# Two graph layers on one core: decoding edge counts in pairs, with the weights stored by parity of the node

## The chip, the core and the metric

The kernel runs on one core of one Trainium2 chip. A core has TensorE (matmuls into PSUM), VectorE, ScalarE, GpSimd, SyncE (which issues most of the DMAs) and 16 DMA engines. The metric is the device time of one execution in microseconds, from the first to the last work on the chip; the smaller, the better. The time before is the median of three runs.

## The reference

There are N = 3327 nodes with D = 64 features, and a symmetric 0/1 matrix `adj` with about 16 edges in a row. Two layers follow each other, each with a layer norm and a relu in front and a residual sum behind it.

```python
h = relu(layernorm(x))
# layer 0: hyperbolic attention over the edges
att = sigmoid(left[:, None] + right[None, :] + b) * adj
support[i] = sum_j att[i, j] * logmap(h[i], h[j])
x = x + proj(expmap(h, support))
# layer 1: each row's edges are weighted by how many edges stand behind them in the row
h = relu(layernorm(x)); support = h @ weight
rank = cumsum(adj != 0, axis=1); deg = rank[:, -1:]; k = min(deg, 100)
w = mask * where(rank - (deg - k) > 0, 0.5 ** (deg - rank), 0)
x = x + w @ support + bias
```

So an edge's weight in layer 1 is a power of two whose exponent is a count: the number of edges behind it in its row. The last edge of a row has weight 1, the one before it 1/2, and so on.

## The kernel before

**Tiles.** The nodes are padded to 3328, that is 26 blocks of 128. A node j (the source of an edge) lies on a partition, 128 nodes of block j at a time; the nodes i (the rows of the result) lie along the free dimension. Layer 0 walks over four strips of i, with 8, 8, 6 and 4 blocks (1024, 1024, 768 and 512 columns), and inside a strip over the 26 blocks j from the last to the first. A round works on 1024 elements per partition at most: one block j in the first three strips, two in the fourth.

**A round of layer 0.** SyncE loads the part of the adjacency (`ad`). TensorE forms the pair products in PSUM (`products`, L670 and L671), ScalarE puts them through two gelus (`gelus`, L857 and L858) and makes the attention by a tanh (`sigmoids`, L653), and VectorE joins them (`pair_one`, L658, and `pair_two`, L663). TensorE sums the result over j (`total`, L680).

**The counts.** Beside that, in the same rounds, VectorE makes a 0/1 mask of the edges (`edges`, L620), and TensorE counts the edges behind each place in one PSUM tile that goes on from block to block (`count`, L631 and L632). `read` then takes the count out of PSUM, clips it at zero and keeps it. A count is one byte, in `behind_lo` (blocks 0 to 11) and `behind_hi` (blocks 16 to 25). The four blocks of `JD` (12 to 15) are different: their counts are multiplied by 128 at once and kept as 16 bit words in `weight_of`. A word of 128 * count, read as a bfloat16, has the count as its exponent, so it is the weight itself, up to a fixed power of two. `ON_ACT` says which reads ScalarE takes (L642); VectorE takes the others (L644 for the blocks of `JD`, L646 otherwise).

**Behind the strips.** After each strip a chain of small steps (`post`, in `per_node`) closes layer 0 for its nodes: sums, roots by GpSimd's power operation, the tanh, the new `x_sb`, the layer norm, and at its end the features `s2` (L1147, L1149) that layer 1 multiplies with. For the first three strips GpSimd does the small steps while the next strip runs; for the last strip VectorE does them (all recorded at L1044), during layer 1. The chain is a generator that yields after each step with a cost; `advance(LAST)` lets it go on by 8 units for each block of layer 1.

**Layer 1.** `weights` takes the blocks j in the order 12 to 15, 0 to 11, 16 to 21, and last the four blocks 22 to 25 that belong to the last strip. `decode` turns a block's 128 x 3328 bytes into words: ScalarE by a copy with a factor of 128 (L1285), VectorE by a product with 128 (L1287), in turn. It runs four blocks ahead of the matmuls (`LEAD`), into seven buffers `wt`. For each block `add` (L1299) makes seven matmuls, one for each chunk of 512 columns (the last has 256), with `s2` as the weights of the array, into seven PSUM tiles `pw`. For the last four blocks the order turns: chunk by chunk, all four blocks. Behind each chunk, ScalarE or VectorE copies `pw` to `ow` (L1340, L1342), and two chunks later `close` multiplies it by the layer's weight matrix (`w2s`, L1328), adds `x_sb` (which holds the bias already, L1304) and sends 512 rows out by a DMA.

**Order.** The order of work on TensorE, VectorE and ScalarE is the order in which the program issues it (`manual_schedule(engines=IN_ORDER)`): an instruction that waits holds up all that stands behind it on its engine. GpSimd and the DMAs on SyncE's queue follow their own orders. A branch to a general version of the kernel (not taken here) stands at the end.

Of the kernel before, what the change touches and what calls it, by code (L numbers as in the profile page):

```python
# [11 lines left out]
F32 = mybir.dt.float32  # L12
F16 = mybir.dt.float16
BF16 = mybir.dt.bfloat16
I32 = mybir.dt.int32
U16 = mybir.dt.uint16
U8 = mybir.dt.uint8
AF = mybir.ActivationFunctionType
ALU = mybir.AluOpType
# [3 lines left out]
P = 128  # L23
N = 3327
NB = 26
NP = NB * P
D = 64
# [3 lines left out]
JD = range(12, 16)  # L31
# [9 lines left out]
ROUND = (3.5, 3.5, 2.8, 1.9)  # L41

LEAD = 4

GSTRIPS = [(0, 7), (7, 7), (14, 6), (20, 6)]
GFMAX = 7 * P
# [35 lines left out]
def halves(n):  # L82
    return [(a, min(a + 512, n)) for a in range(0, n, 512)]
# [363 lines left out]
def fast(ctx, tc, x, adj_t, r, w_att, b_att, weight, bias, out, flag):  # L447

    nc = tc.nc
    V, A, G, T = nc.vector, nc.scalar, nc.gpsimd, nc.tensor  # L450
    const = ctx.enter_context(tc.tile_pool(name="f_const", bufs=1))

    x_sb = const.tile([P, NB, D], F32, name="x_sb")
# [14 lines left out]
    w2s = const.tile([P, D], F32, name="w2s")  # L468
# [67 lines left out]
    weight_of = const.tile([P, len(JD), NP], U16, name="weight_of")  # L536
    s2 = const.tile([P, NB, 2, D], F16, name="s2")
# [7 lines left out]
    def behind(j):  # L545
        if j in JD:
            return weight_of[:, j - JD.start]
        return behind_of["lo"][:, j] if j < JD.start else behind_hi[:, j - JD.stop]
# [53 lines left out]
    def span(n):  # L602
        k, lo, hi = rounds[n]
        return (hi - lo) * strips[k].F
# [17 lines left out]
    def count(n, j):  # L622
# [9 lines left out]
            T.matmul(S.pc[:, f0:f1], cb, now[:, f0:f1], start=S.first, stop=True, skip_group_check=True)  # L632
        S.before, S.first = now, False

    def read(n, j, on_act=None):
        k, lo, hi = rounds[n]
        S = strips[k]
        kept = behind(j)[:, S.i0 : S.i0 + S.F]
        num, den = ON_ACT[k]
        i = NB - 1 - j  # L640
        if on_act or (on_act is None and i * num // den != (i + 1) * num // den):
            A.activation(kept, S.pc[:, : S.F], AF.Relu, scale=128.0 if j in JD else 1.0)  # L642
        elif j in JD:
            V.tensor_scalar(kept, S.pc[:, : S.F], 0.0, 128.0, op0=ALU.max, op1=ALU.mult)  # L644
        else:
            V.tensor_scalar(kept, S.pc[:, : S.F], 0.0, None, op0=ALU.max)  # L646

# [58 lines left out]
    d, rl, sq, sr = (pre.tile([P, NB, D], F32, name=n) for n in ("d", "rl", "sq", "sr"))  # L706
# [3 lines left out]
    for hs in node_halves:  # L710
        n = hs.stop - hs.start
# [166 lines left out]
    for j in js(0):  # L878
        read(0, j, True)
# [10 lines left out]
    for b in (24, 20, 16, 12, 8, 4, 0):  # L890
        n = min(4, NB - b)
# [23 lines left out]
    for j in js(1):  # L915
        read(1, j, True)
# [251 lines left out]
    def per_node(k, pa):  # L1168
        nb = STRIPS[k][1]
        agg = post_pool.tile([P, nb, D + 1], F32, name="agg_last" if k + 1 == len(STRIPS) else "agg")  # L1170
        for c in range(0, nb, 4):
            m = min(4, nb - c)
            to, of = agg[:, c : c + m], pa[:, c * P : c * P + m * (D + 1)].rearrange("p (b d) -> p b d", b=m)
            if c == 0:
                V.tensor_copy(to, of)
            else:
                A.copy(to, of)
        return post(agg, k)
# [5 lines left out]
    def advance(portions):  # L1184
        for stage in stages:
            while portions > 0 and not stage.asked:
                portion = next(stage.portions, LATER)
                stage.asked = portion == ACT
                if portion >= LATER:
                    break  # L1190
                portions -= portion

    def asked_of_act():
        for stage in stages:
            if stage.asked:
                next(stage.portions)
                stage.asked = False

    def finish():
        for stage in stages:  # L1200
            for _ in stage.portions:
                pass
        stages.clear()
# [5 lines left out]
    for n in range(2, R):  # L1209
        k, lo, hi = rounds[n]  # L1210
        m, w = n + AHEAD, span(n)
# [22 lines left out]
        if n == 2:  # L1234
            for j in js(2):
                read(2, j, True)
# [33 lines left out]

    late = STRIPS[-1][0]
    order = [*JD, *range(JD.start), *range(JD.stop, late)]
    chunks = halves(NP)
    with tc.tile_pool(name="l1", bufs=2, reuse_waits="tile") as l1, tc.manual_schedule(engines=IN_ORDER):
        decoded = 0

        def decode(j):

            nonlocal decoded
            if j in JD:  # L1280
                return behind(j)
            wt = l1.tile([P, NP], U16, name="wt", bufs=7)
            decoded += 1
            if decoded % 2:
                A.activation(wt, behind(j), AF.Copy, scale=128.0)  # L1285
            else:
                V.tensor_scalar(wt, behind(j), 128.0, None, op0=ALU.mult)  # L1287
            return wt

        every = [*order, *range(late, NB)]  # L1290
        weights = {j: decode(j) for j in every[: len(JD) + 1]}
        stages.append(Stage(per_node(len(STRIPS) - 1, pa)))
        sums.close()
        l1_ps = ctx.enter_context(tc.tile_pool(name="l1_ps", bufs=1, space=PSUM, reuse_waits="tile"))
        pw = [l1_ps.tile([P, f1 - f0], F32, name=f"pw{n}") for n, (f0, f1) in enumerate(chunks)]

        def add(j, wt, n):
            f0, f1 = chunks[n]
            T.matmul(pw[n], s2[:, j].rearrange("p c d -> p (c d)"), wt[:, f0:f1].bitcast(BF16),  # L1299
                     start=j == order[0], stop=j == NB - 1)  # L1300

        def bias(b0, nb):
            xb = x_sb[:, b0 : b0 + nb]
            G.tensor_add(xb, xb, bias_b[:, None, :].to_broadcast([P, nb, D]))  # L1304

        for i, j in enumerate(order):
            for jn in every[: i + 1 + LEAD]:
                if jn not in weights:
                    weights[jn] = decode(jn)
            asked_of_act()  # L1310
            advance(LAST)
            for n in range(len(chunks)):
                add(j, weights[j], n)
            if i % 4 == 3 and i < STRIPS[-2][0]:
                bias(i - 3, 4)
        finish()
        bias(STRIPS[-2][0], late - STRIPS[-2][0])
        bias(late, NB - late)
        for j in range(late, NB):
            if j not in weights:  # L1320
                weights[j] = decode(j)
        ow = [l1.tile([P, 512], F32, name="ow", bufs=4)[:, : f1 - f0] for f0, f1 in chunks]

        def close(n):
            f0, f1 = chunks[n]
            b0, nb = f0 // P, (f1 - f0) // P
            for b in range(nb):
                T.matmul(pw[n][:, b * D : (b + 1) * D], ow[n][:, b * P : (b + 1) * P], w2s, start=True, stop=True)  # L1328
            o = l1.tile([P, 4, D], F32, name="o", bufs=4)
            V.tensor_add(o[:, :nb], pw[n][:, : nb * D].rearrange("p (b d) -> p b d", d=D), x_sb[:, b0 : b0 + nb])  # L1330
            full = nb if b0 + nb < NB else nb - 1
            nc.sync.dma_start(out[f0 : f0 + full * P, :].rearrange("(b p) d -> p b d", p=P), o[:, :full])
            if full < nb:
                nc.scalar.dma_start(out[f0 + full * P : N, :], o[: N - f0 - full * P, full])

        for n in range(len(chunks)):
            for j in range(late, NB):
                add(j, weights[j], n)
            if n % 2:
                A.copy(ow[n], pw[n])  # L1340
            else:
                V.tensor_copy(ow[n], pw[n])  # L1342
            if n > 1:
                close(n - 2)
        close(len(chunks) - 2)
        close(len(chunks) - 1)


@with_exitstack
def gnn_kernel(  # L1350
    ctx: ExitStack,
    tc: tile.TileContext,
    x: bass.AP,
    adj_t: bass.AP,
    r: bass.AP,
    w_att: bass.AP,
    b_att: bass.AP,
    weight: bass.AP,
    bias: bass.AP,
    out: bass.AP,  # L1360
):
    keep = ctx.enter_context(tc.tile_pool(name="keep", bufs=1))
    flag = keep.tile([1, 1], I32, name="flag")
    args = (x, adj_t, r, w_att, b_att, weight, bias, out)
    with ExitStack() as inner:
        fast(inner, tc, *args, flag)
    cond = tc.nc.values_load(flag)
    with tc.If(cond > 0):
        with ExitStack() as inner:
            general(inner, tc, *args)  # L1370
# [28 lines left out]
```

## Time and profile before

| | before |
|---|---|
| median of 3 runs (lowest, highest) | 416.37 us (414.42, 418.77) |
| the profiled execution: its time / its span | 418.25 us / 416.4 us |
| mean granted TensorE clock | 0.969 |
| busy: TensorE / VectorE / ScalarE / GpSimd | 361.1 / 373.1 / 364.8 / 124.0 us |
| first matmul of layer 1 | at 360.26 us |
| decodings: ScalarE / VectorE | 11 of 2.96 us / 11 of 1.89 us |
| reads of a `JD` block with 1024 columns: ScalarE / VectorE | 1.01 / 1.21 us |
| end of the last matmul / last output DMA issued | about 409.2 / 409.8 us |

The span runs from the first to the last instruction of the profiled execution. Times in the profile are microseconds unless marked ns. "PE" is TensorE's matmuls, "PEld" its loads of array weights, "DVE" VectorE, "ACT" ScalarE, "POOL" GpSimd, "SP" SyncE. A row gives the line in the kernel, the operation, what is written and what is read, and a shape. An idle time is given with the work that ended it. The chain of work that ended last is followed back from the last instruction. The granted clock is the share of full speed that TensorE had. Ends of matmuls are modelled.

### The profile page before, as it was taken

What the parts mean: (1) busy time and instruction counts of PE and PEld (TensorE: products, weight loads), DVE (VectorE), ACT (ScalarE), POOL (GpSimd) and SP (SyncE); (2) the same over time, 40 slices, a digit from 0 to 9 for tenths busy, and PEclk for the clock granted to TensorE, in tenths of its full rate; (3) what the DMA queues carried; (4) which work ended last, traced back from release to release, by engine and by line L of the source; (5) the groups of instructions that cost most, each with busy time, mean ns of one, the idle gap of its engine ahead of it and who ended that gap; (6) DMA issues with size and microseconds to landing.
All of it is one profiled execution on the core that took longest, in us unless ns stands there. A gap on an engine that the chain in (4) does not pass through costs nothing.

```text
span 416.4 us, 4699 instructions
## 1 busy us (share of the span) xinstructions
PE 361.1 (87%) x1436; PEld 154.4 (37%) x1460; DVE 373.1 (90%) x546; ACT 364.8 (88%) x411; POOL 124.0 (30%) x240
## 2 busy tenths in 40 slices
PE   0088999999997999999997999999777999899793
PEld 0063333333333333333333444444332333344352
DVE  4999799999999899999999798899989899898841
ACT  3589999999998899999999899999996999788810
POOL 8154200000000263930250163801405183452400
PEclk9998999999999899999999899999898999999987
DMA  7315544545466534554437255454643420000012
GB/s 218 123 40 143 161 148 147 158 145 161 146 186 181 152 107 148 153 151 109 145 113 178 94 153 151 119 146 128 186 117 104 114 87 0 2 0 0 2 25 65
DMA packets 23298, 48.99 MB, mean 118 GB/s; under 512 B 8789, under 2 KB 9245, under 8 KB 23265
## 3 DMA queue, kind: packets, MB, share of 16 engines
q1 hardware_dynamic: 20993, 47.66, 39.2%
q10 hardware_dynamic: 1808, 0.46, 0.6%
q0 software_dynamic: 464, 0.49, 0.5%
q8 instruction: 13, 0.21, 0.2%
q14 instruction: 20, 0.16, 0.1%
HBM read 46.40 MB, written 0.87 MB: 114 GB/s over the span
## 4 chain that ended last, share of the span: by engine, by line
DVE 33%; ACT 27%; PE 24%; issue 10%; POOL 3%; DMA 1%; DVEq 0%; POOLq 0%; ACTq 0%
DVE sg L663 9%; PE po L680 9%; ACT sg L653 8%; DVE sg L658 8%; ACT pq L857 8%; ACT pq L858 3%; DVE wt L1287 3%; PE pq L670 3%; PE pq L671 3%; DVE behind_lo L646 3%; PE pc L632 2%; PE pc L631 2%; ACT behind_lo L642 2%; ACT behind_hi L642 2%; PE pw L1299 2%
## 5 line engine op out<-in xcount | busy, mean ns | idle before, releaser
L680 PE MATMUL po<-sg,hw 128*65 128x512 f32 (+1 forms) x364 | 164.5, 576 | 0.5 <-DVE st L972 0.4
L663 DVE SCALAR_TENSOR_TENSOR sg<-pq,sg 128x1024 f32<-128x1024 f32 (+1 forms) x91 | 103.4, 1137 | 6.7 <-ACT pq L858 5.9
L658 DVE SCALAR_TENSOR_TENSOR sg<-sg,ad 128x1024 f32<-128x1024 f32 (+1 forms) x91 | 103.8, 1141 | 0.3
L653 ACT ACTIVATE sg<-left_b,right 128x1024 f32<-128x1024 f32 (+2 forms) x103 | 99.5, 979 | 0.0
L857 ACT ACTIVATE pq<-pq 128x1024 f32<-128x1024 f32 (+1 forms) x91 | 87.1, 957 | 3.5 <-PE pq L671 3.2
L858 ACT ACTIVATE pq<-pq 128x1024 f32<-128x1024 f32 (+1 forms) x91 | 86.2, 947 | 2.9
L680 PEld LDWEIGHTS po<-sg,hw 128*65 128x65 f32 x364 | 50.4, 141 | 71.3 <-issue 57.5
L631 PE MATMUL pc<-mask,ca 128*128 128x512 bf16 (+1 forms) x170 | 62.1, 365 | 11.1 <-DVE behind_hi L646 3.9
L670 PE MATMUL pq<-iu,ju 71*128 71x512 f16 (+1 forms) x182 | 68.2, 375 | 2.4 <-ACT jz L794 1.0
L671 PE MATMUL pq<-iz,jz 128*128 128x512 f16 (+1 forms) x182 | 67.2, 376 | 0.0
L632 PE MATMUL pc<-mask,cb 128*128 128x512 bf16 (+1 forms) x168 | 60.1, 368 | 2.2 <-ACT behind_lo L642 1.7
L620 DVE TENSOR_SCALAR mask<-ad 128x1024 bf16<-128x1024 f32 (+1 forms) x91 | 58.6, 645 | 0.0
L1044 POOL TENSOR_TENSOR dots<-dots,ih 128x8 f32<-128x8 f32 (+1 forms) x3 | 2.2, 720 | 134.3 <-DVE dots L1064 134.3
L1299 PE MATMUL pw<-wt,s 128*128 128x512 bf16 (+1 forms) x150 | 33.6, 374 | 4.3 <-DVE s L1149 2.2
L632 PEld LDWEIGHTS <-cb 128*128 128x128 bf16 x182 | 17.9, 98 | 51.7 <-issue 39.8
L631 PEld LDWEIGHTS <-ca 128*128 128x128 bf16 x175 | 17.3, 99 | 29.9 <-issue 17.8
L670 PEld LDWEIGHTS <-ju 71*128 71x128 f16 x182 | 18.1, 99 | 24.2 <-DVE sg L663 5.8
L1299 PEld LDWEIGHTS <-s 128*128 128x128 f16 x182 | 18.0, 100 | 23.6 <-issue 4.2
L642 ACT ACTIVATE behind_hi<-pc 128x1024 uint8<-128x1024 f32 (+2 forms) x25 | 21.8, 872 | 5.3 <-remote 3.3
L671 PEld LDWEIGHTS <-jz 128*128 128x128 f16 x182 | 18.2, 100 | 19.7 <-issue 3.3
L1304 POOL TENSOR_TENSOR x_sb<-x_sb,bias_b 128x256 f32<-128x256 f32 (+1 forms) x6 | 9.9, 1657 | 51.6 <-DVE w L1133 46.0
L642 ACT ACTIVATE behind_lo<-pc 128x1024 uint8<-128x1024 f32 (+2 forms) x29 | 24.9, 859 | 0.0
(313 smaller groups left out, 369.0 us busy)
## 6 DMA issues: line engine op xcount, KB each, us to landing
ad<-in_adj_t SPq DMA_DIRECT2D x65, 512.0 KB, 3.7
ad<-in_adj_t SPq DMA_DIRECT2D x26, 384.0 KB, 3.2
out<-o SPq DMA_DIRECT2D x6, 128.0 KB, 1.9
left_b<-left_d SPq DMA_DIRECT2D x1, 512.0 KB, 4.6
x_sb<-in_x ACTq DMA_DIRECT2D x1, 416.0 KB, 5.6
x_sb<-in_x SPq DMA_DIRECT2D x1, 416.0 KB
left_b<-left_d SPq DMA_DIRECT2D x1, 384.0 KB
jz<-iz POOLq DMA_DIRECT2D x2, 128.0 KB, 2.6
```

The source lines that it names most:

```text
L631: T.matmul(S.pc[:, f0:f1], ca, S.before[:, f0:f1], start=False, stop=True, skip_group_check=True)
L632: T.matmul(S.pc[:, f0:f1], cb, now[:, f0:f1], start=S.first, stop=True, skip_group_check=True)
L642: A.activation(kept, S.pc[:, : S.F], AF.Relu, scale=128.0 if j in JD else 1.0)
L653: A.activation(part(n, sg, j), S.left[:, : S.F], AF.Tanh, bias=right[:, j : j + 1], scale=0.5)
L658: V.scalar_tensor_tensor(sg, sg, 1.0, ad_of.pop(n)[:, :w], op0=ALU.add, op1=ALU.mult)
L663: V.scalar_tensor_tensor(sg, pq_of.pop(n)[:, :w], WD, sg, op0=ALU.add, op1=ALU.mult)
L670: T.matmul(part(n, pq, j, f0, f1), ju[:KB, j, :], S.iu[:, f0:f1], start=True, stop=False)
L671: T.matmul(part(n, pq, j, f0, f1), jz[:, j, :], S.iz[:, f0:f1], start=False, stop=True)
L680: T.matmul(S.po[: D + 1, f0:f1], hw[:, j, :], part(n, sg_of[n], j, f0, f1), start=j == NB - 1, stop=j == 0)
L857: A.activation(pq, pq, AF.Gelu, scale=-WG / QS)
L858: A.activation(pq, pq, AF.Gelu, scale=WH)
L1299: T.matmul(pw[n], s2[:, j].rearrange("p c d -> p (c d)"), wt[:, f0:f1].bitcast(BF16), start=j == order[0], stop=j == NB - 1)
```

## The change

**Layout by parity.** A row of 3328 weights is now stored as two halves of 1664: first the even nodes i, then the odd ones (`by_parity`). This holds for `weight_of`, which `read` writes in layer 0 from the same counts in PSUM, and for the buffers `wt`.

**Decoding.** VectorE takes two neighbouring bytes as one 16 bit word. One instruction keeps the low byte and shifts it left by 7, which gives the words of the even nodes; a second one keeps the high byte and shifts it right by 1, which gives those of the odd nodes. ScalarE still makes all 3328 words in one instruction, with a source that steps by two bytes. ScalarE now takes one decoding in three (`ACT_DECODES`), so 8 of the 22, and VectorE takes 14.

**Chunks.** The seven chunks of layer 1 keep their sizes, but the first six are now (q, r): the nodes of parity r among the 1024 nodes of group q. The seventh holds both parities of the last 256 nodes. After the sums, `copied` puts the results back in the order of the nodes: the even ones by VectorE, the odd ones by ScalarE, each with a step of two in its destination `kept_of`. `close` then works on a group of 1024 nodes and so waits for both of its chunks.

```diff
@@ -41,6 +41,7 @@
 ROUND = (3.5, 3.5, 2.8, 1.9)
 
 LEAD = 4
+ACT_DECODES = 3
 
 GSTRIPS = [(0, 7), (7, 7), (14, 6), (20, 6)]
 GFMAX = 7 * P
@@ -632,16 +633,23 @@
             T.matmul(S.pc[:, f0:f1], cb, now[:, f0:f1], start=S.first, stop=True, skip_group_check=True)
         S.before, S.first = now, False
 
+    def by_parity(t):
+        return t.rearrange("p (r k) -> p r k", r=2)
+
     def read(n, j, on_act=None):
         k, lo, hi = rounds[n]
         S = strips[k]
         kept = behind(j)[:, S.i0 : S.i0 + S.F]
         num, den = ON_ACT[k]
         i = NB - 1 - j
+        of = S.pc[:, : S.F]
+        if j in JD:
+            kept = by_parity(weight_of[:, j - JD.start])[:, :, S.i0 // 2 : (S.i0 + S.F) // 2].rearrange("p r k -> p k r")
+            of = of.rearrange("p (k r) -> p k r", r=2)
         if on_act or (on_act is None and i * num // den != (i + 1) * num // den):
-            A.activation(kept, S.pc[:, : S.F], AF.Relu, scale=128.0 if j in JD else 1.0)
+            A.activation(kept, of, AF.Relu, scale=128.0 if j in JD else 1.0)
         elif j in JD:
-            V.tensor_scalar(kept, S.pc[:, : S.F], 0.0, 128.0, op0=ALU.max, op1=ALU.mult)
+            V.tensor_scalar(kept, of, 0.0, 128.0, op0=ALU.max, op1=ALU.mult)
         else:
             V.tensor_scalar(kept, S.pc[:, : S.F], 0.0, None, op0=ALU.max)
 
@@ -1270,7 +1278,8 @@
 
     late = STRIPS[-1][0]
     order = [*JD, *range(JD.start), *range(JD.stop, late)]
-    chunks = halves(NP)
+    chunks = [(q, r) for q in range(3) for r in range(2)] + [(3, None)]
+    widths = [512] * 6 + [256]
     with tc.tile_pool(name="l1", bufs=2, reuse_waits="tile") as l1, tc.manual_schedule(engines=IN_ORDER):
         decoded = 0
 
@@ -1281,10 +1290,13 @@
                 return behind(j)
             wt = l1.tile([P, NP], U16, name="wt", bufs=7)
             decoded += 1
-            if decoded % 2:
-                A.activation(wt, behind(j), AF.Copy, scale=128.0)
+            to = by_parity(wt)
+            if decoded % ACT_DECODES == 1:
+                A.activation(to, behind(j).rearrange("p (k r) -> p r k", r=2), AF.Copy, scale=128.0)
             else:
-                V.tensor_scalar(wt, behind(j), 128.0, None, op0=ALU.mult)
+                pairs_of = behind(j).bitcast(U16)
+                V.tensor_scalar(to[:, 0], pairs_of, 0xFF, 7, op0=ALU.bitwise_and, op1=ALU.logical_shift_left)
+                V.tensor_scalar(to[:, 1], pairs_of, 0xFF00, 1, op0=ALU.bitwise_and, op1=ALU.logical_shift_right)
             return wt
 
         every = [*order, *range(late, NB)]
@@ -1292,11 +1304,12 @@
         stages.append(Stage(per_node(len(STRIPS) - 1, pa)))
         sums.close()
         l1_ps = ctx.enter_context(tc.tile_pool(name="l1_ps", bufs=1, space=PSUM, reuse_waits="tile"))
-        pw = [l1_ps.tile([P, f1 - f0], F32, name=f"pw{n}") for n, (f0, f1) in enumerate(chunks)]
+        pw = [l1_ps.tile([P, f], F32, name=f"pw{n}") for n, f in enumerate(widths)]
 
         def add(j, wt, n):
-            f0, f1 = chunks[n]
-            T.matmul(pw[n], s2[:, j].rearrange("p c d -> p (c d)"), wt[:, f0:f1].bitcast(BF16),
+            q, r = chunks[n]
+            w = by_parity(wt.bitcast(BF16))[:, :, 512 * q : min(512 * q + 512, NP // 2)]
+            T.matmul(pw[n], s2[:, j].rearrange("p c d -> p (c d)"), w if r is None else w[:, r],
                      start=j == order[0], stop=j == NB - 1)
 
         def bias(b0, nb):
@@ -1319,31 +1332,41 @@
         for j in range(late, NB):
             if j not in weights:
                 weights[j] = decode(j)
-        ow = [l1.tile([P, 512], F32, name="ow", bufs=4)[:, : f1 - f0] for f0, f1 in chunks]
-
-        def close(n):
-            f0, f1 = chunks[n]
-            b0, nb = f0 // P, (f1 - f0) // P
-            for b in range(nb):
-                T.matmul(pw[n][:, b * D : (b + 1) * D], ow[n][:, b * P : (b + 1) * P], w2s, start=True, stop=True)
-            o = l1.tile([P, 4, D], F32, name="o", bufs=4)
-            V.tensor_add(o[:, :nb], pw[n][:, : nb * D].rearrange("p (b d) -> p b d", d=D), x_sb[:, b0 : b0 + nb])
-            full = nb if b0 + nb < NB else nb - 1
-            nc.sync.dma_start(out[f0 : f0 + full * P, :].rearrange("(b p) d -> p b d", p=P), o[:, :full])
-            if full < nb:
-                nc.scalar.dma_start(out[f0 + full * P : N, :], o[: N - f0 - full * P, full])
+        kept_of = [l1.tile([P, min(NP - 1024 * q, 1024)], F32, name="ow" if q < 3 else "ow_last", bufs=2 if q < 3 else 1)
+                   for q in range(4)]
+
+        def copied(n):
+            q, r = chunks[n]
+            to = kept_of[q].rearrange("p (k r) -> p r k", r=2)
+            if r is None:
+                V.tensor_copy(to, by_parity(pw[n]))
+            elif r == 0:
+                V.tensor_copy(to[:, 0], pw[n])
+            else:
+                A.copy(to[:, 1], pw[n])
+
+        def close(q):
+            for h in range(0, 8 if q < 3 else 2, 4):
+                b0 = 8 * q + h
+                nb = min(4, NB - b0)
+                pc = pw[2 * q + h // 4]
+                for b in range(nb):
+                    T.matmul(pc[:, b * D : (b + 1) * D], kept_of[q][:, (h + b) * P : (h + b + 1) * P], w2s, start=True, stop=True)
+                o = l1.tile([P, 4, D], F32, name="o", bufs=4)
+                V.tensor_add(o[:, :nb], pc[:, : nb * D].rearrange("p (b d) -> p b d", d=D), x_sb[:, b0 : b0 + nb])
+                full = nb if b0 + nb < NB else nb - 1
+                f0 = b0 * P
+                nc.sync.dma_start(out[f0 : f0 + full * P, :].rearrange("(b p) d -> p b d", p=P), o[:, :full])
+                if full < nb:
+                    nc.scalar.dma_start(out[f0 + full * P : N, :], o[: N - f0 - full * P, full])
 
         for n in range(len(chunks)):
             for j in range(late, NB):
                 add(j, weights[j], n)
-            if n % 2:
-                A.copy(ow[n], pw[n])
-            else:
-                V.tensor_copy(ow[n], pw[n])
-            if n > 1:
-                close(n - 2)
-        close(len(chunks) - 2)
-        close(len(chunks) - 1)
+            copied(n)
+            if n > 0 and n % 2 == 0:
+                close(n // 2 - 1)
+        close(3)
 
 
 @with_exitstack
```

## The prediction

> **What bounds the kernel now.** I read the chain that ended last first, then the timeline of the last 60 us, then the groups of the two steps that the change touches. The chain of the page:
>
> ```profile
> DVE 33%; ACT 27%; PE 24%; issue 10%; POOL 3%; DMA 1%; DVEq 0%; POOLq 0%; ACTq 0%
> ```
>
> No one engine owns the time. Up to 357 us (the four strips) VectorE and ScalarE are busy 333 and 331 us of 357 by the windows view, so what either is given there is paid for. From 360 us (layer 1) the engines stand like this at the end, by the timeline (start, duration, engine, line, names, shapes, idle before and its releaser):
>
> ```profile
> 389.94 2.97 PE L1299 MATMUL pw<-wt,s 128*128 128x512 bf16 x13
> ...
> 392.82 1.89 DVE L1287 TENSOR_SCALAR wt<-behind_hi 128x3328 uint16<-128x3328 uint8 x1
> 394.62 0.42 DVE L1149 TENSOR_TENSOR s<-w_last,s 128x256 f16<-128x256 f32 x1
> 394.95 1.89 DVE L1287 TENSOR_SCALAR wt<-behind_hi 128x3328 uint16<-128x3328 uint8 x1
> 395.10 0.60 PE L1299 MATMUL pw<-wt,s 128*128 128x512 bf16 x2 [2.19 <-DVE s L1149]
> 396.27 0.38 PE L1299 MATMUL pw<-wt,s 128*128 128x512 bf16 x1 [0.57 <-ACT wt L1285]
> 396.89 3.47 PE L1299 MATMUL pw<-wt,s 128*128 128x512 bf16 x9 [0.25 <-DVE wt L1287]
> ```
>
> TensorE has finished 22 of the 26 blocks at 392.9 and then stands for VectorE: the last strip's features (L1149) and the last decoding (L1287) come at 395.0 and 396.8. VectorE is late because decodings lie between the steps of its per-node chain. The windows view adds a second cost of this pause (columns: us, busy us and instructions of PE, PEld, DVE, ACT, POOL, then the granted clock, DMA share, GB/s):
>
> ```profile
> 393.00:395.00 2.00, 0.00 (x0) 0.00 (x0) 2.00 (x3) 2.00 (x2) 0.00 (x0) 1.00 0.00 0
> ...
> 397.00:398.50 1.50, 1.50 (x6) 0.55 (x5) 0.69 (x1) 0.00 (x0) 0.00 (x0) 0.66 0.00 0
> 398.50:400.40 1.90, 1.90 (x7) 0.99 (x6) 0.00 (x1) 0.59 (x1) 0.00 (x0) 0.50 0.00 0
> 400.40:402.00 1.60, 1.60 (x12) 1.25 (x12) 1.11 (x2) 0.00 (x0) 0.00 (x0) 0.85 0.00 0
> ```
>
> After the pause the clock is 0.66, 0.50 and 0.85: 0.51 + 0.95 + 0.24 = 1.7 us lost.
>
> The groups of the two steps, by tile (decodings; then the weights that are written in layer 0 already):
>
> ```profile
> L1285 ACT ACTIVATE wt<-behind_lo x6: 2959/2960/2972, 354.8 to 374.6; 128x3328 uint16<-128x3328 uint8 x6
> L1287 DVE TENSOR_SCALAR wt<-behind_lo x6: 1884/1889/1896, 361.6 to 378.4; 128x3328 uint16<-128x3328 uint8 x6
> ```
>
> ```profile
> L642 ACT ACTIVATE weight_of<-pc x9: 583/801/1015, 71.5 to 329.7; 128x1024 uint16<-128x1024 f32 x4, 128x768 uint16<-128x768 f32 x3, 128x512 uint16<-128x512 f32 x2
> L644 DVE TENSOR_SCALAR weight_of<-pc x7: 679/1212/1224, 68.7 to 327.9; 128x1024 uint16<-128x1024 f32 x4, 128x512 uint16<-128x512 f32 x2, 128x768 uint16<-128x768 f32 x1
> ```
>
> **What the Trainium skill says.** "VectorE: DVE Perf Modes", perf-mode tier table: a tensor_scalar whose two sides are 2 bytes wide and in SBUF makes four elements a cycle, others two. The trace agrees for two: 3328 elements in 1.89 us are 1733 ns at two per 0.96 GHz cycle and 156 ns fixed. It has no row at four. "SBUF — State Buffer", Specifications: lines have 16 bytes, and full rate needs two hits per line. The trace leans that way, as shown below. The same page, "SBUF: two separate sides": a VectorE operation that uses two ports and a GpSimd operation shut each other out. The trace agrees: the power operation of the per-node chain took 1.35 us at 343.8 and 2.35 to 2.86 us where a decoding ran beside it. "TensorE: Matmul & The Clock Gate", Part 1: the clock halves after an idle window; the 0.50 above is that.
>
> **The change, part by part.**
>
> *Decoding on VectorE.* One instruction of 3328 elements becomes two of 1664, 16 bit on both sides. At four a cycle one is 1664 / 4 / 0.96 = 433 ns + 156 = 0.59 us. Instructions that follow each other overlap by 0.09 (L1287 shows 1.80 on the chain for 1.89), so a decoding is about 1.0 us instead of 1.8. At two a cycle it would be 2.0, at one 3.8; I take 1.0, since the mode goes by the widths, and the shift at L512 and the product at L513 of the same shape both took 190 ns.
>
> *The share.* Counting 1, 4, 7 ... 22, ScalarE decodes 8 of 22 instead of 11, VectorE 14 instead of 11. ScalarE: 8 x 2.96 = 23.7 us instead of 32.6. Its source now steps by 2 bytes, eight hits per line; I price that at nothing. ScalarE then has 3 us for each 4.2 us of matmuls. If the stepped read doubled it (6 us), ScalarE would need 47 us in a stage of 31: some 15 us late.
>
> *When TensorE ends the 22 blocks.* The first four ran 360.26 to 365.88, 1.405 us each. 22 of them end at 391.15, if no decoding is late (before: 1.6 us of stalls).
>
> *When the last strip's features come.* VectorE's stretch from 360.46 to 395.04 is 34.6 us, with 10 decodings of 1.8. Left are 16.6 us, of which 2.0 are waits for GpSimd. 14 decodings of 1.0 give 16.6 + 14 = 30.6, so 391.1. The power operations get shorter (shorter locks) but are covered less; I call that even, at 391.3. Buffers do not stop it: seven weights are held, and the decoding of block 25 waits for block 18, which ends at 387.
>
> *The end.* TensorE goes on at 391.4. Before, it stood at 396.89 with three of the 28 late matmuls done (0.65 us), which is worth 396.24. So 4.84 us, and 1.7 of the clock if a pause under 1 us does not lower it: 6.5. The closing now waits for both parities of 1024 nodes: the odd copy by ScalarE (0.59) lies under the next chunk's four matmuls (0.86), except at the last group, whose cover is 0.44 us and which waits some 0.3 to 0.4. The copies write with a step of 8 bytes, two hits per line; if each cost half as much again it would be 0.3 more. I take 0.5 in all. Output DMAs stay seven on SP and one on ScalarE's queue, of the same sizes, behind the same additions. Gain: 6.5 - 0.5 = 6.0 us. It is 3.5 if the clock falls anyway and the features come half a microsecond later, and 6.7 at best.
>
> *Writing the four blocks' weights in layer 0 (L642, L644).* Same 16 instructions and elements, but neighbours now land 1664 words apart, so that each element goes to another line than the one before. No large row of before does this. The nearest are small ones: `hw[:, :, D] = opx * wn`, 26 floats 260 bytes apart, beside its neighbour with plain writes:
>
> ```profile
> L888 DVE TENSOR_TENSOR hw<-opx,wn x1: 206/206/206, 28.4 to 28.4; 128x26 f32<-128x26 f32 x1
> L889 DVE TENSOR_TENSOR wn<-wn,y x1: 188/188/188, 28.6 to 28.6; 128x26 f32<-128x26 f32 x1
> ```
>
> Against 182 (the mean of such products, 172 to 188) that is 24 / 26 = 0.9 ns per element more. L810 writes 26 places 156 bytes apart (52 elements) in 230 where 52 plain ones take 190: 1.5 ns per place. L812, stepped in source and result, took 272: 90 / 26 = 3.4. The bounds are 0 and 3.4; nothing excludes 0, since a longer instruction is not the same as a longer short one, but a gain is excluded, since the elements stay as many. I take 1.2 (the middle of 0.9 and 1.5) for both engines; for ScalarE no row shows it. What lies on the path: of the 16 reads the chain goes through 8: two of 1024 in the first strip (one on each engine), two of 1024 in the second, three of 768 in the third and one of 512 in the fourth, for instance
>
> ```profile
> 166.70 1.01 ACT weight_of L642
> 170.72 0.91 ACT weight_of L642
> ```
>
> That is 4096 + 2304 + 512 = 6912 elements x 1.2 = 8.3 us. The other 8 lie beside the other engine's longer work; without that cover all 13,312 elements would give 16.0. Behind a longer read wait TensorE's next count (one PSUM tile) and, on the same engine, the next gelu or pair product.
>
> *Sum.* 418.25 (span 416.4 and 1.85 around it) + 8.3 - 6.0 = 420.6. This execution was 1.9 above the median of the three runs, 416.37, so 418.7 is the forecast.
>
> **The rivals.**
> A, *the stepped writes cost nothing.* For it: the one or two cycles of small rows may be start-up. Then only the 6.0 stay: 410.4, faster by 1.4%. The balance is at 6.0 / 6912 = 0.87 ns per element.
> C, *the stepped writes cost like L812*, 2 to 3.4 ns: 6912 to 13,312 elements give 14 to 45 us, less 6.0: 424 to 455, around 436. It is slower; it decides from 1.5 ns on (10.2 us, less 6.0). Against it: L812 steps on both sides.
> D, *a decoding doesn't get faster*: at one element a cycle VectorE has 14 x 3.7 = 52 us of decodings in the stretch of 34.6, which ends at 360.46 + 16.6 + 52 = 429 instead of 395: +34 and the writes' 8.3, about 458. At two a cycle: 16.6 + 28 gives 405, +10, about 435. Against it: L512 and L513.
> Layer 1 could also stay with ScalarE's stepped read (above); that goes with D.
>
> **How the numbers follow.** Forecast (B) 0.50, with its own range 414.5 to 424 (0.65 to 2.0 ns, gain 3.5 to 6.7); A 0.25; C 0.16; D 0.09. A difference under about 1% (4.2 us) can't be told from none. Faster by over 1%: nearly all of A, 0.23. Within: the rest of A and six tenths of B, 0.33. Slower: the rest of B, C and D, 0.44. The range runs from A's 410.4, less 0.9 for its best gain, to 430, which cuts off D and the upper half of C, under 2 in 10.
>
> **What would show it.** L1287 replaced by pairs of about 0.59 us, 28 of them; TensorE's pause at the end of the 22 blocks under 1 us and a clock of 1.0 through the closing; the writes of weight_of with 1024 elements at about 2.4 us on VectorE and 2.2 on ScalarE (before 1.21 and 1.01), and the start of layer 1's first matmul moved from 360.3 to about 368.6. If that start stays at 360, A holds. If the pairs take 1 us or more each, or ScalarE's decodings more than 3 us, D does, and the whole sum is wrong.

## The result and the profile after

The changed kernel takes 448.76 us (median of four runs, 447.33 to 449.47), the kernel before beside it 416.55: a ratio of 1.076, with a 95% interval of 1.072 to 1.080. It is 32 us slower. The forecast was 418.7, in a range up to 430. The profiled execution took 449.47 us, with a span of 447.8.

The groups on the page of the changed kernel name the place at once (line, engine, operation, count, then busy us, mean ns, idle time before and its releaser):

```profile
L650 ACT ACTIVATE weight_of<-pc 128x1024 uint16<-128x1024 f32 (+2 forms) x9 | 34.5, 3838 | 7.4 <-PE pc L633 4.1
L652 DVE TENSOR_SCALAR weight_of<-pc 128x1024 uint16<-128x1024 f32 (+2 forms) x7 | 27.1, 3877 | 10.9 <-PE pc L633 5.9
```

These are the 16 reads of the `JD` blocks. They have the same elements as before and were 7.6 and 7.2 us in all; now they are 34.5 and 27.1, 46.8 us more. The view by tile says how one of them changed (ns, least/median/most) and who waits for it (us, times):

```profile
L650 ACT ACTIVATE weight_of<-pc x9: 2447/3609/4747, 75.6 to 364.7; 128x1024 uint16<-128x1024 f32 x4, 128x768 uint16<-128x768 f32 x3, 128x512 uint16<-128x512 f32 x2
L652 DVE TENSOR_SCALAR weight_of<-pc x7: 2408/4669/4696, 69.4 to 361.6; 128x1024 uint16<-128x1024 f32 x4, 128x512 uint16<-128x512 f32 x2, 128x768 uint16<-128x768 f32 x1
...
  PE pc L632: 30.7, 16
```

A read of 1024 columns went from 1.01 and 1.21 us to 4.7 on both engines: 3.6 and 3.4 ns per element more. TensorE's next count stands 30.7 us for them, before 1.1. The chain of work in the first strip shows how they come to lie on the path (start, duration, engine, tile and line):

```profile
69.37 4.68 DVE weight_of L652
74.05 0.04 issue
74.09 0.38 PE pc L632
74.47 0.23 PE pc L633
74.70 0.87 PE pc L632
75.56 0.02 issue
75.59 4.75 ACT weight_of L650
80.34 0.04 issue
80.38 0.38 PE pc L632
80.75 0.22 PE pc L633
80.97 0.22 PE pc L632
81.19 0.23 PE pc L633
```

Count, read, count, read: there is one PSUM tile of counts, so the four reads of the first strip follow each other at 5.8 to 6.2 us (4.7 for the read and 1.1 for the count and the handing over), although they lie on two engines. Before, they were 2.8 to 4.1 us apart, the pace of the other work:

```profile
68.70 1.22 DVE L644 TENSOR_SCALAR weight_of<-pc 128x1024 uint16<-128x1024 f32 x1
...
71.50 1.01 ACT L642 ACTIVATE weight_of<-pc 128x1024 uint16<-128x1024 f32 x1
...
75.57 1.21 DVE L644 TENSOR_SCALAR weight_of<-pc 128x1024 uint16<-128x1024 f32 x1
...
78.64 1.01 ACT L642 ACTIVATE weight_of<-pc 128x1024 uint16<-128x1024 f32 x1
```

In the second and the third strip two of the four reads follow each other on ScalarE. The chain of the third strip (768 columns) runs through ScalarE's own order there instead, read, two gelus (`pq`), tanh (`sg`), read:

```profile
275.98 3.46 ACT weight_of L650
279.45 0.71 ACT pq L865
...
281.91 3.47 ACT weight_of L650
```

These two start 5.9 us apart, before 3.2; the two of the second strip 7.7, before 3.9. In each case the whole of the longer read came on top. So there were two ways onto the path, the one tile of counts and the engine's own order. In the end layer 1's first matmul comes at 397.04 us instead of 360.26: 36.8 of the 46.8 us are on the path.

From there on the change does what it was made for. The decodings:

```profile
L1298 DVE TENSOR_SCALAR wt<-behind_lo x8: 576/584/594, 398.4 to 413.1; 128x1664 uint16<-128x1664 uint16 x8
L1299 DVE TENSOR_SCALAR wt<-behind_lo x8: 575/583/587, 398.9 to 413.6; 128x1664 uint16<-128x1664 uint16 x8
L1295 ACT ACTIVATE wt<-behind_lo x4: 2961/2965/2972, 391.6 to 407.7; 128x3328 uint16<-128x3328 uint8 x4
```

The last strip's features, and TensorE from the first matmul of layer 1 to its last one, by the timeline:

```profile
424.73 0.41 DVE L1157 TENSOR_TENSOR s<-w_last,s 128x256 f16<-128x256 f32 x1
```

```profile
397.04 5.78 PE L1312 MATMUL pw<-weight_of,s 128*128 128x512 bf16 x27
402.66 28.03 PE L1312 MATMUL pw<-wt,s 128*128 128x512 bf16 x135
...
437.71 2.00 PE L1354 MATMUL pw<-w2s,ow 128*128 128x64 f32 x16 [0.31 <-ACT ow L1346]
439.54 0.61 PE L1354 MATMUL pw<-w2s,ow_last 128*128 128x64 f32 x4
```

The features are there at 425.1, before TensorE needs them at 427.9 (22 blocks of 1.405 us after 397.04), and the matmuls run on without a pause until 430.7. The granted clock stays at 1.00 in every stretch of layer 1 up to 440.2, where before it fell to 0.50. From layer 1's first matmul to the end of its last one are 43.2 us, before 49.0.

### The profile page after: what moved, and what is told of

It reads as the page before. It is cut to its first block, busy times and chain, and to the rows that moved or that the text cites. A ratio compares the mean times of both kernels' runs of the same rounds, so it can differ in the third digit from the quotient of the medians.

```text
span 447.8 us, 4713 instructions
## 1 busy us (share of the span) xinstructions
PE 364.8 (81%) x1436; PEld 154.3 (34%) x1460; DVE 386.8 (86%) x563; ACT 384.3 (86%) x408; POOL 113.7 (25%) x240
## 4 chain that ended last, share of the span: by engine, by line
DVE 32%; ACT 30%; PE 23%; issue 13%; DMA 1%; DVEq 0%; ACTq 0%
DVE sg L671 9%; DVE sg L666 9%; PE pw L1312 8%; ACT pq L865 7%; ACT sg L661 7%; ACT weight_of L650 6%; DVE weight_of L652 5%; ACT pq L866 4%; PE po L688 4%; PE pc L632 3%; ACT behind_lo L650 3%; PE pc L633 2%; DVE mask L621 2%; PE pq L678 2%; DVE behind_hi L654 1%
## 5 line engine op out<-in xcount | busy, mean ns | idle before, releaser
L671 DVE SCALAR_TENSOR_TENSOR sg<-pq,sg 128x1024 f32<-128x1024 f32 (+1 forms) x91 | 105.2, 1156 | 11.4 <-ACT pq L866 10.8
L865 ACT ACTIVATE pq<-pq 128x1024 f32<-128x1024 f32 (+1 forms) x91 | 90.6, 996 | 4.3 <-PE pq L679 3.9
L866 ACT ACTIVATE pq<-pq 128x1024 f32<-128x1024 f32 (+1 forms) x91 | 86.2, 947 | 2.9
L678 PE MATMUL pq<-iu,ju 71*128 71x512 f16 (+1 forms) x182 | 69.8, 383 | 2.3 <-ACT jz L802 1.0
L679 PE MATMUL pq<-iz,jz 128*128 128x512 f16 (+1 forms) x182 | 68.4, 382 | 0.0
L633 PE MATMUL pc<-mask,cb 128*128 128x512 bf16 (+1 forms) x168 | 61.6, 376 | 2.1 <-ACT behind_lo L650 1.7
L650 ACT ACTIVATE weight_of<-pc 128x1024 uint16<-128x1024 f32 (+2 forms) x9 | 34.5, 3838 | 7.4 <-PE pc L633 4.1
L652 DVE TENSOR_SCALAR weight_of<-pc 128x1024 uint16<-128x1024 f32 (+2 forms) x7 | 27.1, 3877 | 10.9 <-PE pc L633 5.9
L1312 PE MATMUL pw<-wt,s 128*128 128x512 bf16 (+1 forms) x150 | 31.0, 363 | 0.2
L1317 POOL TENSOR_TENSOR x_sb<-x_sb,bias_b 128x256 f32<-128x256 f32 (+1 forms) x6 | 8.3, 1393 | 74.1 <-DVE w L1141 68.2
```

The lines of the kernel that those rows point to most:

```text
L650: A.activation(kept, of, AF.Relu, scale=128.0 if j in JD else 1.0)
L671: V.scalar_tensor_tensor(sg, pq_of.pop(n)[:, :w], WD, sg, op0=ALU.add, op1=ALU.mult)
L678: T.matmul(part(n, pq, j, f0, f1), ju[:KB, j, :], S.iu[:, f0:f1], start=True, stop=False)
L679: T.matmul(part(n, pq, j, f0, f1), jz[:, j, :], S.iz[:, f0:f1], start=False, stop=True)
L865: A.activation(pq, pq, AF.Gelu, scale=-WG / QS)
L866: A.activation(pq, pq, AF.Gelu, scale=WH)
```

## The experiments

All ratios are to the kernel before, with a 95% interval where there is one. The half by half version is the base of most. Executions of the kernel before lay between 413.9 and 420.9 us, so a single run, or a start of layer 1 read from the one profiled execution of a version, can be off by two or three microseconds.

**The same bytes, written half by half.**

```diff
-            kept = by_parity(weight_of[:, j - JD.start])[:, :, S.i0 // 2 : (S.i0 + S.F) // 2].rearrange("p r k -> p k r")
-            of = of.rearrange("p (k r) -> p k r", r=2)
+            kept = by_parity(weight_of[:, j - JD.start])[:, :, S.i0 // 2 : (S.i0 + S.F) // 2]
+            of = of.rearrange("p (k r) -> p r k", r=2)
```

> The changed kernel, but the reads of the four JD blocks walk their 1024 columns half by half: all even columns, then all odd ones, so that each half is written without gaps and PSUM is read in steps of two. The stored bytes are the same. Theory (what cost 37 us is that neighbouring elements land in different places): a read takes 1.0 us on ScalarE and 1.2 on VectorE again, layer 1 starts at about 360, and the gain of layer 1 (43.2 us from its first to its last matmul, before 49.0) is left: 410.7 us, faster by 1.4%. Rival (the step through PSUM costs as much as the step in SBUF): reads of 2 to 4.7 us, 425 to 449 us. Rival (the layout itself costs, whoever writes it): 449 us.

Measured: 409.96 us, ratio 0.985 (0.981 to 0.990). It is faster than both kernels. Its reads by tile:

```profile
L650 ACT ACTIVATE weight_of<-pc x9: 582/800/1016, 72.0 to 327.5; 128x1024 uint16<-128x1024 f32 x4, 128x768 uint16<-128x768 f32 x3, 128x512 uint16<-128x512 f32 x2
L652 DVE TENSOR_SCALAR weight_of<-pc x7: 677/1222/1226, 69.2 to 325.7; 128x1024 uint16<-128x1024 f32 x4, 128x512 uint16<-128x512 f32 x2, 128x768 uint16<-128x768 f32 x1
```

They cost what they cost before, and layer 1 starts at 358.0. Only the order in which the elements of one instruction are walked differs from the changed kernel, so this order is the whole loss: 38.8 us between the two versions. The layout is not to blame, and a read of PSUM in steps of two floats is free (1.016 and 1.226 us at most, before 1.015 and 1.224).

**What a stepped write costs.** This kernel leaves both layers out and writes 1024 elements in different patterns, for instance

```diff
+    V.tensor_scalar(W[:, :, :512].rearrange("p r k -> p k r"), alt, 0.0, 128.0, op0=ALU.max, op1=ALU.mult)
...
+    V.tensor_scalar(s2[:, 0:4096:4], pc, 0.0, 128.0, op0=ALU.max, op1=ALU.mult)
```

> Does none of the layers: it loads x, turns 1024 columns of it into PSUM and writes them out by VectorE and ScalarE, one after the other, in 21 patterns of 1024 elements, then returns x. Prices in us for VectorE / ScalarE. Theory L (an element costs more when it lands in another 16 byte line than the one before): 16 bit words plain 1.2 / 1.0, alternating between two halves 4.7 / 4.7, in steps of 2 or 4 words little more than plain, from 8 words on 4.7; floats in steps of 2 little, from 4 on and alternating 4.7; runs of 2, 4, 8 words 3.0, 2.1, 1.7. Rival N (any word narrower than four bytes that has no neighbour costs): 16 bit in steps of 2 already 4.7, floats plain price in every pattern, bytes dearest. Rival R (rows of two elements in the pattern cost, not the places): only the alternating patterns 4.7, one-dimensional steps of any size plain; runs of 2 as dear as alternating, runs of 8 nearly plain.

Its groups by shape, from one run (busy us, mean ns): VectorE's rows, and ScalarE's only for L88. L47 is plain 16 bit words, L49 alternating halves, L53, L55, L57 and L59 steps of 2, 4, 8 and 16 words; L63 and L65 floats in steps of 2 and 4, L69 floats alternating; L73 and L77 bytes in steps of 4 and alternating; L79 alternating runs of two words; L85 and L87 plain and alternating words from SBUF, L88 the latter by ScalarE. All other rows read PSUM:

```profile
L88 ACT ACTIVATE to<-x_sb 128x1024 uint16<-128x1024 f32 x1 | 4.7, 4712 | 2.8 <-DVE to L87 2.8
L77 DVE TENSOR_SCALAR to<-pc 128x1024 uint8<-128x1024 f32 x1 | 4.7, 4704 | 4.8 <-ACT to L76 4.8
...
L57 DVE TENSOR_SCALAR to<-pc 128x1024 uint16<-128x1024 f32 x1 | 4.7, 4680 | 2.5 <-ACT to L56 2.5
...
L49 DVE TENSOR_SCALAR to<-pc 128x1024 uint16<-128x1024 f32 x1 | 4.7, 4668 | 1.1 <-ACT to L48 1.1
...
L59 DVE TENSOR_SCALAR to<-pc 128x1024 uint16<-128x1024 f32 x1 | 4.4, 4426 | 4.8 <-ACT to L58 4.8
L87 DVE TENSOR_SCALAR to<-x_sb 128x1024 uint16<-128x1024 f32 x1 | 2.7, 2745 | 1.1 <-ACT to L86 1.1
...
L55 DVE TENSOR_SCALAR to<-pc 128x1024 uint16<-128x1024 f32 x1 | 2.4, 2420 | 1.4 <-ACT to L54 1.4
...
L65 DVE TENSOR_SCALAR to<-pc 128x1024 f32<-128x1024 f32 x1 | 1.9, 1950 | 1.1 <-ACT to L64 1.1
...
L69 DVE TENSOR_SCALAR to<-pc 128x1024 f32<-128x1024 f32 x1 | 1.9, 1917 | 2.1 <-ACT to L68 2.1
...
L53 DVE TENSOR_SCALAR to<-pc 128x1024 uint16<-128x1024 f32 x1 | 1.3, 1292 | 1.1 <-ACT to L52 1.1
...
L73 DVE TENSOR_SCALAR to<-pc 128x1024 uint8<-128x1024 f32 x1 | 1.3, 1291 | 1.1 <-ACT to L72 1.1
...
L63 DVE TENSOR_SCALAR to<-pc 128x1024 f32<-128x1024 f32 x1 | 1.2, 1225 | 1.1 <-ACT to L62 1.1
...
L79 DVE TENSOR_SCALAR to<-pc 128x1024 uint16<-128x1024 f32 x1 | 1.2, 1224 | 4.8 <-ACT to L78 4.8
...
L47 DVE TENSOR_SCALAR to<-pc 128x1024 uint16<-128x1024 f32 x1 | 1.2, 1211 | 0.0
...
L85 DVE TENSOR_SCALAR to<-x_sb 128x1024 uint16<-128x1024 f32 x1 | 0.7, 694 | 1.1 <-ACT to L84 1.1
```

From PSUM, ScalarE's rows differ from VectorE's by under 0.02 us wherever the write is what costs, so this price is not that of one engine. It does not go by the pattern of the write alone either: from SBUF the alternating write takes VectorE 2.75 us and ScalarE still 4.71. Why VectorE is quicker there, this run does not show.

None of the three theories holds whole. Count how often a write comes to another 16 byte line than the one before. Single 16 bit words come to 1024 lines (steps of 8 words, or alternating), 512 (steps of 4) or 256 (steps of 2), and take 4.68, 2.42 and 1.29 us. These three lie on one straight line: 4.41 ns for each visit to a line and 0.16 us once (an estimate from the three). Steps of 16 words come to as many lines as steps of 8; they take 0.25 us less, which stays open, but not more, while steps of 4 words take half: the three fit a line of 16 bytes, and none of 8 or 32. Single bytes cost the same as single words: 1.29 us in steps of 4, which are 256 visits, and 4.70 alternating.

Floats that come to 1024 lines take 1.92 to 1.95 us, so about 1.75 ns a visit beside the same 0.16. At 512 visits (steps of 2) that makes 1.06 us: VectorE's plain write, 1.22, hides it, and ScalarE, whose plain write takes 1.02, takes 1.07. Runs of two words, four bytes without a gap, come to 512 lines too and cost VectorE nothing, where single words in steps of 4 put the same four bytes into each line, in two pieces, and cost 2.42. So a visit whose pieces are narrower than four bytes costs two and a half times one that writes four bytes whole.

Theory L has the line right and the sizes wrong. Theory N is right that narrow writes are dear and wrong that floats are free and that steps of 2 are dear. Theory R falls: one-dimensional steps are as dear as the alternating rows.

**One engine at a time.** In the half by half version, the reads of one engine alternate again:

```diff
+            if not on_a:
+                kept, of = (t.rearrange("p r k -> p k r") for t in (kept, of))
```

> The changed kernel with only VectorE's seven JD reads alternating between the halves; ScalarE's nine go half by half. VectorE's seven cost 20 us more than plain ones. If the whole excess is on the path: 410.7 + 20 = 431 us. If the excess is shared as in the changed kernel (36.8 of 47): 426 to 427. If half by half is no cheaper: 449.

Measured (one run): 427.39 us, 17.4 more than half by half; layer 1 starts at 375.0, 17.0 later.

The other engine (`if on_a`):

> The changed kernel with only ScalarE's nine JD reads alternating; VectorE's seven go half by half. ScalarE's nine cost 27 us more than plain ones. If the whole excess is on the path: 438 us; shared as in the changed kernel: 431 to 432. The two runs' excesses over the first one add up to some 37 us if reads on the two engines do not cover each other (a read on one engine holds up the next on the other through the single PSUM tile of counts), and to clearly more if they did.

Measured (one run): 437.56 us, 27.6 more; layer 1 starts 27.1 later. VectorE's 19.9 us of longer reads are on the path by 17.0, ScalarE's 26.9 by all. The two excesses add up to 45.0, against 38.8 when both engines alternate: reads on the two engines cover each other by some 6 us, a rough figure from single runs.

With one engine slow the way onto the path can be another one than the count. In the first strip the chain goes on from the first slow read to the same engine's next work: to the pair product on VectorE (first pair of lines, VectorE alternating), to the gelu on ScalarE (second pair, ScalarE alternating):

```profile
68.48 4.68 DVE weight_of L655
73.16 1.05 DVE sg L674
```

```profile
71.67 4.71 ACT weight_of L653
76.38 0.93 ACT pq L868
```

**A smaller price.** Inside each half every fourth word is written first, then their neighbours:

```diff
+            of = of.rearrange("p (a b r) -> p r b a", r=2, b=4)
+            kept = kept.rearrange("p r (a b) -> p r b a", b=4)
```

> The half by half version, but inside a half every fourth word is written first, then the ones beside them, and so on: the stored bytes are the same, and two elements follow each other in a 16 byte line. The prices of the small run give 2.4 us for 1024 elements on both engines, that is 1.2 to 1.4 ns per element more than plain: the size that the prediction took. It tells how much of such a cost lies on the path. The prediction's count (the 8 reads that lie on the chain of the kernel before, 6912 elements): 8 to 9 us over the half by half version, 418.5 us. Everything on the path (13,312 elements): 17 us, 427 us. The share of the alternating kernel (38.8 of 47): 14 us, 424 us.

Measured: 420.95 us, ratio 1.009 (1.007 to 1.012). Its reads take 2.43 to 2.46 us for 1024 columns and in all 17.4 us more than plain ones; layer 1 starts at 368.4, 10.4 later than in the half by half version. So 60% is on the path, between the prediction's 52% and the 79% of the changed kernel (83% when it is held against the half by half version too). The tile answer and TensorE's waits:

```profile
L651 ACT ACTIVATE weight_of<-pc x9: 1293/1872/2465, 72.4 to 337.2; 128x1024 uint16<-128x1024 f32 x4, 128x768 uint16<-128x768 f32 x3, 128x512 uint16<-128x512 f32 x2
L653 DVE TENSOR_SCALAR weight_of<-pc x7: 1283/2422/2451, 68.9 to 334.9; 128x1024 uint16<-128x1024 f32 x4, 128x512 uint16<-128x512 f32 x2, 128x768 uint16<-128x768 f32 x1
...
  PE pc L632: 10.3, 10
```

A read of 2.4 and 1.1 for the count make 3.5 us, about a round of the first strip (4.0 and 2.9 in turn from one pair product to the next, 3.4 in the mean). That the share grows with the price follows from these two runs. That it does so because, above a round, the loop of count and read sets the pace is an argument from the durations, and not tested apart from the engine's own order.

**The decoding's two parts.** The half by half version with ScalarE and VectorE in turn again:

```diff
-ACT_DECODES = 3
+ACT_DECODES = 2
```

> The half by half version with the decodings shared in turn again, 11 on ScalarE and 11 pairs on VectorE. Theory (layer 1 is now bound by TensorE alone, 43 us without a pause): ScalarE needs 11 x 2.97 = 32.7 us beside 31 us of matmuls, so it may come late by a microsecond or two at the end: 410 to 412 us. Rival (the share of a third is what the gain hangs on): back near 415.

Measured: 411.07 us, ratio 0.987 (0.983 to 0.990), not to be told from the half by half version.

Both parts undone, with

```diff
-                V.tensor_scalar(to[:, 0], pairs_of, 0xFF, 7, op0=ALU.bitwise_and, op1=ALU.logical_shift_left)
-                V.tensor_scalar(to[:, 1], pairs_of, 0xFF00, 1, op0=ALU.bitwise_and, op1=ALU.logical_shift_right)
+                V.tensor_scalar(to, behind(j).rearrange("p (k r) -> p r k", r=2), 128.0, None, op0=ALU.mult)
```

> The half by half version with both parts of the decoding undone: one product of 3328 elements on VectorE, its source in steps of two bytes, and 11 decodings on each engine. The parity layout, the chunks and the closing stay. Theory (layout and closing are free, the gain is the decoding's): the kernel before, 416.5 us. Rival (the closing by groups of 1024 gains or loses something itself): 414 or 418.5.

Measured: 418.01 us, ratio 1.004 (1.001 to 1.007), nearer to the rival's 418.5 than to the 416.5 expected. Its pauses before the last blocks are those of the kernel before (L1310 is `add`, L1352 the closing):

```profile
394.64 0.61 PE L1310 MATMUL pw<-wt,s 128*128 128x512 bf16 x2 [2.19 <-DVE s L1157]
395.82 0.38 PE L1310 MATMUL pw<-wt,s 128*128 128x512 bf16 x1 [0.57 <-ACT wt L1295]
396.44 3.45 PE L1310 MATMUL pw<-wt,s 128*128 128x512 bf16 x9 [0.25 <-DVE wt L1297]
...
407.13 2.00 PE L1352 MATMUL pw<-w2s,ow 128*128 128x64 f32 x16 [0.31 <-ACT ow L1344]
```

So layout, chunks and closing bring nothing; they cost 0.1 to 0.7%, of which the last line shows 0.31 us.

Only the product back, the share kept:

> The half by half version with one product per decoding on VectorE (1.8 us instead of two times 0.5) but the share kept: 8 on ScalarE, 14 on VectorE. VectorE's stretch in layer 1 gets 14 x 0.8 = 11 us longer, so TensorE waits some 9 us for the last strip's features and its clock falls: 420 to 421 us. If VectorE had that much slack: 410.

Measured (one run): 424.27 us, 3 above the expectation. Layer 1 itself takes 54.0 us, 10.8 more than half by half, as expected; TensorE's waits (6.0 us for VectorE's weights, 1.9 for the last strip's features) lie in part inside the 22 blocks. The 3 us lie ahead of that: layer 1 starts at 360.9 instead of 358.0, which the decoding does not explain, and which lies within what single runs differ by. The four versions say it together: with pairs the share makes no difference that can be measured, without them a third for ScalarE is worse than half. The gain is the pairs': 1.004 against 0.987 at the same share, some 7 us.

**Node order kept for the four blocks.**

```diff
-            kept = by_parity(weight_of[:, j - JD.start])[:, :, S.i0 // 2 : (S.i0 + S.F) // 2]
-            of = of.rearrange("p (k r) -> p r k", r=2)
+            kept = weight_of[:, j - JD.start, S.i0 : S.i0 + S.F]
...
-            w = by_parity(wt.bitcast(BF16))[:, :, 512 * q : min(512 * q + 512, NP // 2)]
+            w = wt.bitcast(BF16)
+            w = w.rearrange("p (k r) -> p r k", r=2) if j in JD else by_parity(w)
+            w = w[:, :, 512 * q : min(512 * q + 512, NP // 2)]
```

> The half by half version with the four JD blocks kept in the order of the nodes, as in the kernel before; TensorE picks the parity by reading their words in steps of two. If TensorE streams words four bytes apart at its full rate: 410 us, and the first four blocks of layer 1 take 5.6 us. If it reads such words at half rate: those 28 matmuls take 11 us, 415.5 us.

Measured: 410.99 us, ratio 0.988 (0.985 to 0.992), the same as half by half within what can be told. The first four blocks take 5.9 us (358.07 to 363.94) instead of 5.6: TensorE streams words four bytes apart at close to its full rate, so the stride could as well have been left to the reader.

## Why the prediction was wrong

**What failed: the price of a stepped write.** The step "I take 1.2 (the middle of 0.9 and 1.5) for both engines" measured 3.4 on VectorE and 3.6 on ScalarE. The prediction had the right row beside it and set it aside. The small run's figures reproduce both kinds of row: 0.16 us and 26 visits of 4.41 ns make 0.27 to 0.28 us for L812, which writes 26 single 16 bit words and took 0.272; with 1.75 ns a visit they make 0.21 us for L888, which writes 26 floats and took 0.206. So L888 shows the price of floats, 0.7 ns per element more than plain in the small run (1.95 against 1.22 us). L812 shows that of the reads; its surplus is 90 / 26 = 3.5, where the prediction wrote 3.4. L810 has two elements in most of its lines and, like L87, a single source in SBUF (L812 reads SBUF too, from two sources, and is not cheaper). The prediction put L812 down to its stepped source, and took the middle of two rows that differ from the reads in width or in visits. The Trainium skill's line rule, "SBUF — State Buffer", Specifications, points to the place but not to the size: two hits per line are enough for floats here (1.22 us) and not for 16 bit words (2.42).

**What failed with it: the share on the path.** The chain of the kernel before names the side that is late today; eight of 16 reads were on it. At 1.2 to 1.4 ns that count is nearly right (10.4 us measured beside 8.3 forecast, for a total of 17.4 where the prediction had 16.0), and the run by fours ends near the forecast, at 420.95 beside 418.7. At the true price it is not: 6912 x 3.5 = 24 us would have been counted, some 435 us in all; 36.8 came. The prediction names both ways onto the path: behind a longer read "wait TensorE's next count (one PSUM tile) and, on the same engine, the next gelu or pair product". But it put the eight reads that were off the chain at nothing, and did not work out what happens once a read and a count together outlast a round.

**What held.** Each instruction of a pair was put at 0.59 us and took 0.58. ScalarE's stepped source costs nothing (2.96 us). TensorE's 22 blocks ran without a stall. The wait at the last closing was put at 0.3 to 0.4 us and is 0.31; the clock does not fall. The copies in steps of two floats cost what the small run gives (VectorE 0.69 us as before, ScalarE 0.62 instead of 0.59). The whole gain of layer 1 was put at 6.0 us and is 5.8 between first and last matmul. Only the last strip's features came earlier than worked out, 28.1 us after layer 1's start instead of 31. GpSimd's three powers for them took 1.30 to 1.46 us instead of 2.35 to 2.59, 3.3 us less in all, which fits, though it was not tested; the prediction had called shorter locks and less cover even. It brings nothing, since TensorE has work until 427.9.

**The rivals.** C, a price like L812's, is what happened: 424 to 455 us forecast, 448.8 measured, with the deciding point at 1.5 ns. A, with plain writes in place of free stepped ones, is what the half by half version makes of the change (410.4 forecast, 409.96 measured). D did not occur.

## What to carry to other kernels

Before a layout is changed, look at each writer of it and at the order in which its instruction walks: a loop order inside one access pattern can cost more than the layout gains, and turning the two loops (or leaving the stride to a reader that doesn't mind) can be free. Price an access pattern by a row that has the same element width, and as many visits to another line, even if it is a row of 26 elements; do not average rows that differ in these, and mind the source too (VectorE's alternating write took 2.7 us from SBUF and 4.7 from PSUM). When a step is made longer, ask what loop it is part of: once it no longer fits into the pace of the rest, most of it is on the path (here 79 to 100%), whatever share of it the chain shows today.

## What was not expected

- From PSUM, a write of single pieces narrower than four bytes costs about 4.4 ns each time it comes to another 16 byte line, on VectorE and ScalarE alike (4.68 and 4.69 us for 1024 words in steps of 8, of which 0.16 is fixed); one of four bytes about 1.75 ns (1.95 us). Where this is less than the plain write takes, it is hidden. Two neighbouring 16 bit words in alternation between two places cost VectorE no more than plain ones (1.22 us).
- Reading PSUM in steps of 2 floats costs nothing on either engine (1.226 and 1.024 us against 1.211 and 1.025); in steps of 8 the reads by fours cost what their writes alone cost (2.42 to 2.46 us).
- The mask and shift of 16 bit words handles 1664 in 0.584 us. Less the 156 ns that the prediction took as fixed, that is 0.26 ns per word, half of the 0.52 of the product of bytes (3328 in 1.89 us).
